# v and tau laid out in DRAM for every channel, Haar coefficients kept at true scale, and mixing's rows loaded a step earlier

## The chip, the cores and the metric

The kernel runs on one core of a Trainium2 chip. The metric is the device time of one execution in microseconds; the kernel before takes 2840.51 us (median of three runs, 2833.68 to 2842.04).

## What is computed

The input x has 4 images of 64 channels of 256 x 256 numbers in fp32. Four layers follow one another. Layers 0, 2 and 3 are long convolutions, layer 1 mixes channels in a Haar wavelet domain:

```python
# layers 0, 2, 3: k is an outer product of two learned filters per channel
y = irfft2(rfft2(x) * rfft2(k))[..., :L, :L]
x = y + x * bias[:, None, None]
# layer 1
f1 = haar2d(x)
acc = 0
for i in range(2):
    f4 = einsum('bchw,oc->bohw', f1 * v[i], conv_w[i])
    acc += sign(f4) * relu(abs(f4) - tau[i])
x = haar2d(acc, inverse=True) + x
```

v and tau have one value for each of the two branches and each of the 256 x 256 coefficients, the same for all channels. conv_w[i] is a 64 x 64 matrix over the channels. The kernel adds x in the Haar domain, so that one inverse transform serves for both. Since v is the same for all channels, it is applied after the channel matrix.

## The kernel before, in words

The filters are separable, so a convolution is two products with triangular Toeplitz matrices, one over rows and one over columns, in blocks of 64 (`toeplitz`, L303, matmuls at L307). A Haar transform of 256 is done as a product of 64 x 64 in the matmuls (`haar`, L316, matmuls at L319) for one axis and as a chain of sums and differences along the free axis for the other (`forward_free`, L334; `inverse_free`, L362).

The images are split in two groups of two. Work goes in rounds of two channels of one group, 32 rounds a group, and there are three phases.

- Phase A (`phase_a`, L427) does layer 0 and the forward transform of a round: load x (L136), products over rows (PSUM a1ps, copied by ScalarE at L451), products over columns (a2ps, with the bias added by VectorE at L471), the free axis on GpSimd (L355 and L357), the other axis on TensorE (a3ps), a copy out of PSUM into f (L484), and a store of f to DRAM as coef (L488).
- Phase B (`phase_b`, L529) mixes the channels of one group. A step takes 128 rows of coefficients, and there are 64 steps; each step has two units, one for each branch. A unit is: `mix` (matmuls with conv_w, L595), `multiply` by v (VectorE, L610), `sign` and `magnitude` (ScalarE, L614 and L618), `less` (minus tau, VectorE, L621), `threshold` (VectorE, L624), `add` (GpSimd, L636 for the second unit of a step, L639 and L640 for the first). ScalarE moves half of the rows with `exchange` (L630). A step loads ft from coef (L550) and v and tau (L556), and stores gt as mixed (L645).
- Phase C (`phase_c`, L692) loads mixed (L704), does the inverse transform, and layers 2 and 3, and stores out.

Transfers are all issued from the sync engine's queue (SP), in program order. Each engine works through its instructions in the order in which the program emits them. That order is written out by hand: every phase is a list of small pieces, and `beside` (L822) emits the pieces of a main phase with those of a side list spread evenly between them. While phase A works on group 1, phase B mixes group 0; while phase C works on group 0, phase B mixes group 1. Phase A of group 0 has the filter networks and their spreading to DRAM beside it (`rest`, L291). Phase C of group 1 runs alone at the end. Evacuations of PSUM in phases A and C are put off by `later` (L401) to the beginning of the next piece.

In phase B, piece (u, j) with j = 0, 1, 2 does the parts of unit u that `piece` (L648) lists: in j = 0 the multiply of u, `less` of u - 1 and `add` of u - 2; in j = 1 the matmuls of u + 1. At j = 1 of a step's first unit the loads of step s + 2 are issued, and at j = 2 of its second unit the store of step s - 1. The buffers are 4 for ft, 3 each for v, tau, m and gt, 2 for x, and one PSUM tile each for the matmul's result and for a.

The Haar butterflies are done without the factors of the square root of a half, and the coefficients lie in DRAM unscaled. Their scale is instead put into tau: `scale_tau` (L264) multiplies tau by the inverse scale along both axes, and `copy_tau` (L271) writes the result to a DRAM tensor, taus, in eight copies. v comes from the host in eight copies too. Both are read with a step of zero over the 8 channels that share a copy:

```python
at = src.offset + s * 4 * W * COPIES
flat = bass.AP(src.tensor, at, [[2 * W, 2 * COPIES], [0, C // COPIES], [1, 2 * W]])
```

The first rows of the transform, which hold sums over all blocks, are treated apart: `join` (L564) at the beginning of mixing, on VectorE, and `part` (L576) before the first store, on GpSimd.

Of the kernel before, what the change touches and what calls it, by code (L numbers as in the profile page):

```python
# [41 lines left out]
F32 = mybir.dt.float32  # L42
AF = mybir.ActivationFunctionType
ALU = mybir.AluOpType
# [3 lines left out]
P = 128  # L48
B, C, N = 4, 64, 256

ROW = 64
# [8 lines left out]

FIRST = 2

COPIES = 8

GROUPS = 2
NB = B // GROUPS
CI = 4 // NB
# [22 lines left out]

@with_exitstack
def conv_haar_kernel(
    ctx: ExitStack, tc: tile.TileContext, x, zT, w1, wbd, cols, decay, wo_first, decay_first, bias, forward, inverse, wcol, wrow, pack, v, tau, out
):
    nc = tc.nc
    ctx.enter_context(tc.manual_schedule())
# [9 lines left out]
    coef = [coefficients(f"coef{g}") for g in range(GROUPS)]  # L106
    mixed = [coefficients(f"mixed{g}") for g in range(GROUPS)]
    filt = [dram.tile([P, REPEATS, PERIOD], F32, tag=f"filt{l}", name=f"filt{l}") for l in range(NL)]

    taus = dram.tile([C, 2, COPIES, 2, W], F32, tag="taus", name="taus")  # L110


    def pool(name, bufs, stack=ctx, **kw):
        return stack.enter_context(tc.tile_pool(name=name, bufs=bufs, reuse_waits="tile", **kw))
# [50 lines left out]
    def constant(name, src, shape):  # L165
        t = mp.tile(shape, F32, tag=name, name=f"{name}_sb")
        nc.sync.dma_start(t, src)
        return t
# [89 lines left out]
    thresholds = []  # L258

    def load_tau():  # L260
        thresholds.append(constant("wrow", wrow.partition_broadcast(P), [P, N]))
        thresholds.append(constant("tau", tau, [P, 4, N]))

    def scale_tau():  # L264
        wrow_sb, tau_sb = thresholds
        nc.vector.tensor_tensor(tau_sb, tau_sb, wrow_sb.unsqueeze(1).to_broadcast([P, 4, N]), ALU.mult)
        for h in range(2):
            half = tau_sb.rearrange("p (i h) k -> p i h k", h=2)[:, :, h, :]
            nc.vector.tensor_scalar(half, half, wcol_sb[:, h : h + 1], None, ALU.mult)

    def copy_tau(k):  # L271
        tau_sb = thresholds[1]
        for i in range(2):
            to = bass.AP(taus.tensor, taus.offset + (k * 2 + i) * W, [[2 * W * COPIES, P], [1, W]])
            nc.sync.dma_start(to, tau_sb[:, 2 * i : 2 * i + 2].rearrange("p h k -> p (h k)"))
# [6 lines left out]
    wcol_sb = const.tile([P, 2], F32, tag="wcol", name="wcol_sb")  # L282
    nc.sync.dma_start(wcol_sb, wcol)
    bias_sb = const.tile([P, NL * C], F32, tag="bias", name="bias_sb")
    nc.sync.dma_start(bias_sb, bias.partition_broadcast(P))

# [1 line left out]
        p()  # L288

    thirds = [slice(0, 7), slice(7, 14), slice(14, REPEATS)]  # L290
    rest = [load_tau] + [lambda q=q, k=k: spread(0, q, k) for q in range(1, 4) for k in thirds]  # L291
# [3 lines left out]
    rest.append(scale_tau)  # L295
    rest += [lambda k=k: copy_tau(k) for k in range(COPIES)]

    TILES = [(r, c) for r in range(2) for c in range(2)]

# [62 lines left out]
    def inverse_free(src, dst, name, engine):  # L362


        blocks = src.rearrange("p n (k q) -> p n k q", k=BLOCKS)

        def diffs(half):
            if half < BLOCKS:
                return blocks[:, :, half : 2 * half, 0]
            m = half // BLOCKS  # L370
            return src.rearrange("p n (k q) -> p (n k) q", k=BLOCKS)[:, :, m : 2 * m]

        def scale(half):
            if half < N and engine is nc.gpsimd:
                nc.scalar.mul(diffs(half), diffs(half), float(half))  # L375

        cur, half = blocks[:, :, 0:1, 0], 1
        while half < N:
            scale(2 * half)
            o = dst  # L380
            if half < HALF:
                o = ac.tile([P, 2 * M, 2 * half], F32, tag=f"h{2 * half}", name=f"{name}{2 * half}", bufs=1)
            d = diffs(half)
            if half < BLOCKS:
                s, pair = cur, o.rearrange("p n (t q) -> p n t q", q=2)
            else:
                s = cur.rearrange("p n (k t) -> p (n k) t", k=BLOCKS)
                pair = o.rearrange("p n (k t q) -> p (n k) t q", k=BLOCKS, q=2)
            for q, op in ((0, ALU.add), (1, ALU.subtract)):
                to = pair[:, :, :, q]  # L390
                if engine is nc.gpsimd:
                    engine.tensor_tensor(to, s, d, op)  # L392
                else:
                    engine.scalar_tensor_tensor(to, d, float(half) * (1 - 2 * q), s, ALU.mult, ALU.add)
                yield
            cur = o
            half *= 2
# [3 lines left out]
    def later(op):  # L401

        waiting.append(op)
# [23 lines left out]
    def phase_a():  # L427
# [45 lines left out]
        def product(t, bp):  # L473
            s = st[t]
            if bp == 0:

                s["f"] = big("out", f"f_{t}", 2)
            two = banks(f"a3ps{bp}_{t}")
            fw = blocks(s["fw"])
            haar(two, lambda r, c: fw[half(r), c, 2 * bp : 2 * bp + 2], forward_sb)  # L480
            for b, ps in enumerate(two):
                f = s["f"][:, 4 * bp + 2 * b : 4 * bp + 2 * b + 2]
                copy = nc.vector.tensor_copy if b and t < ROUNDS else nc.scalar.copy
                later(lambda f=f, ps=ps, copy=copy: copy(f, ps))  # L484

        def store(t):
            for to, f in all_rows(coef[t // ROUNDS], t % ROUNDS, st[t]["f"]):
# [41 lines left out]
    def phase_b(grp):  # L529
# [11 lines left out]
            at = [ap.offset + (e * STEPS // 2 + s // 2) * PAIR + s % 2 * P // CI * n for e in range(CI)]  # L541
            return [(bass.AP(ap.tensor, at[e], [[n, P // CI], [1, n]]), by_e[e]) for e in range(CI)]

        def load(s):
            if s >= STEPS:
                return
            d = st[s]
            d["f"] = bp.tile([P, NB, W], F32, tag="ft", name=f"ft_{grp}_{s}", bufs=4)
            for rows, f in step_of(coef[grp], s, d["f"]):
                nc.sync.dma_start(f, rows)  # L550
            for name, src in (("v", v), ("tau", taus)):
                t = d[name] = bp.tile([P, 2, W], F32, tag=name, name=f"{name}_{grp}_{s}", bufs=3)

                at = src.offset + s * 4 * W * COPIES
                flat = bass.AP(src.tensor, at, [[2 * W, 2 * COPIES], [0, C // COPIES], [1, 2 * W]])
                nc.sync.dma_start(t.rearrange("p e w -> p (e w)"), flat)  # L556

        def four(name, at, b):

# [4 lines left out]
        def join(image):  # L564

            a, b, c, d, t, u = four("f", half(image), image)
            op = nc.vector.tensor_tensor
            op(t, a, b, ALU.add)
            op(b, a, b, ALU.subtract)
            op(u, c, d, ALU.add)  # L570
            op(d, c, d, ALU.subtract)
            nc.vector.tensor_copy(c, b)
            op(a, t, u, ALU.add)
            op(b, t, u, ALU.subtract)

        def part():  # L576

            a, b, c, d, t, u = four("g", half(0), slice(0, NB))
            op = nc.gpsimd.tensor_tensor
            op(t, a, b, ALU.add)  # L580
            op(b, a, b, ALU.subtract)
            op(u, c, c, ALU.add)
            op(a, t, u, ALU.add)
            op(d, d, d, ALU.add)
            op(c, b, d, ALU.add)
            op(d, b, d, ALU.subtract)
            op(b, t, u, ALU.subtract)
# [55 lines left out]
        def store(s):  # L643
            for to, g in step_of(mixed[grp], s, st[s]["g"]):
                nc.sync.dma_start(to, g)  # L645
            st[s].clear()

        def piece(u, j):  # L648

            s, i = divmod(u, 2)  # L650
            if j == 0:
                if u < units:
                    multiply(u)
                if 0 < u <= units:
                    less(u - 1)
                if 1 < u <= units + 1:
                    add(u - 2)
            elif j == 1:
                if u + 1 < units:
                    mix(u + 1)  # L660
                if u < units:
                    sign(u)
                if 0 < u <= units:
                    threshold(u - 1)
                if i == 0 and s > 0:
                    load(s + 2)
            else:
                if u < units:
                    magnitude(u)
                if i == 0 and s < STEPS:  # L670
                    exchange(s)
                if i and s > 0:

                    if s == 2:
                        part()
                        store(0)
                    if s > 1:
                        store(s - 1)
# [12 lines left out]

    def phase_c():  # L692
# [277 lines left out]
```

## Time and profile before

| What | Before |
| --- | --- |
| Time | 2840.51 us (2833.68 to 2842.04) |
| Span of the profiled execution | 2849.9 us, clock of TensorE 0.941 of full |
| TensorE busy | 2429.2 us (85%) |
| VectorE (DVE) busy | 1582.2 us (56%), 1779 instructions |
| ScalarE (ACT) busy | 1427.8 us (50%), 2361 instructions |
| GpSimd (POOL) busy | 1947.6 us (68%), 2422 instructions |
| DMA engines, main queue | 71.5% of 16 engines, 628.64 MB |
| HBM read, written | 413.12 MB, 215.35 MB |

A line of a group in the profile names the source line, the engine, the operation, the output and the inputs, and the count; then the busy time in us, the mean ns of one, the idle time of the engine just before, and what ended most of it. A line of waits names who waited, for whom, the total in us, how many times, and the longest. PEld is the loading of weights. SPq is the sync engine's queue. "issue" is time for which the profile shows no cause. The page gives shares over the whole span; the stages have different limits, so a table of busy time by stretches is read beside it.

### The profile page before, as it was taken

What the parts mean: (1) busy time and instruction counts of PE and PEld (TensorE: products, weight loads), DVE (VectorE), ACT (ScalarE), POOL (GpSimd) and SP (SyncE); (2) the same over time, 40 slices, a digit from 0 to 9 for tenths busy, and PEclk for the clock granted to TensorE, in tenths of its full rate; (3) what the DMA queues carried; (4) which work ended last, traced back from release to release, by engine and by line L of the source; (5) the groups of instructions that cost most, each with busy time, mean ns of one, the idle gap of its engine ahead of it and who ended that gap; (6) DMA issues with size and microseconds to landing.
All of it is one profiled execution on the core that took longest, in us unless ns stands there. A gap on an engine that the chain in (4) does not pass through costs nothing.

```text
span 2849.9 us, 120142 instructions
## 1 busy us (share of the span) xinstructions
PE 2429.2 (85%) x53276; PEld 1931.0 (68%) x53276; DVE 1582.2 (56%) x1779; ACT 1427.8 (50%) x2361; POOL 1947.6 (68%) x2422
## 2 busy tenths in 40 slices
PE   6999998667677676769888888888889999999999
PEld 5777776444444454547676767676667888888888
DVE  2353336777677777527776767676763333333333
ACT  1222224666656566426675666675763333333332
POOL 2787777977778787648777777776765555555561
PEclk9999999988988888879999999999999999999999
DMA  5668887989989998666888888887885444444432
GB/s 156 219 212 262 239 283 245 274 280 283 277 268 294 280 286 276 207 186 195 257 263 244 270 259 240 257 258 230 259 245 184 146 145 149 142 158 134 158 118 93
DMA packets 243773, 636.31 MB, mean 223 GB/s; under 512 B 43174, under 2 KB 125767, under 8 KB 227128
## 3 DMA queue, kind: packets, MB, share of 16 engines
q1 hardware_dynamic: 243256, 628.64, 71.5%
q8 instruction: 419, 6.86, 1.0%
q14 instruction: 98, 0.80, 0.1%
HBM read 413.12 MB, written 215.35 MB: 221 GB/s over the span
## 4 chain that ended last, share of the span: by engine, by line
PE 40%; DMA 23%; DVE 9%; ACT 5%; POOL 4%; issue 3%; SPq 3%; DVEq 0%; ACTq 0%; POOLq 0%
PE c1c L307 8%; PE c2r L307 8%; PE c2c L307 7%; PE c1r L307 6%; DMA ft<-coef 6%; DMA v<-in_v 4%; DMA tau<-taus 4%; PE f L595 3%; PE c0ps L319 3%; DMA x<-in_x 3%; DVE a L621 2%; DMA mixed<-gt 2%; DVE x L610 2%; DMA g<-mixed 2%; PE a2ps L307 1%
## 5 line engine op out<-in xcount | busy, mean ns | idle before, releaser
L392 POOL TENSOR_TENSOR i<-i,g 128x16 f32<-128x16 f32 x744 | 394.5, 550 | 489.3 <-ACT g L375 476.6
L595 PE MATMUL f<-ft,mix 64*64 64x512 f32 x2048 | 341.3, 687 | 262.2 <-DMA ft<-coef 180.5
L610 DVE TENSOR_TENSOR x<-f,v 128x1024 f32<-128x1024 f32 x256 | 312.0, 1219 | 267.0 <-PE f L595 140.4
L307 PEld LDWEIGHTS a1ps<-tx,x 64*64 64x64 f32 x8192 | 322.5, 142 | 121.5 <-issue 61.7
L307 PE MATMUL a1ps<-tx,x 64*64 64x192 f32 (+3 forms) x8192 | 354.2, 315 | 34.6 <-issue 11.2
L614 ACT ACTIVATE m<-x 128x1024 f32<-128x1024 f32 x256 | 272.0, 1063 | 209.9 <-DVE x L610 151.7
L307 PEld LDWEIGHTS c2r<-tx,cy 64*64 64x64 f32 x8192 | 307.6, 137 | 92.0 <-ACT ch L745 53.9
L307 PEld LDWEIGHTS c1c<-ty,ch 64*64 64x64 f32 x8192 | 300.9, 133 | 90.2 <-ACT ch L745 53.1
L307 PEld LDWEIGHTS a2ps<-ty,ay 64*64 64x64 f32 x8192 | 308.1, 140 | 70.8 <-issue 44.3
L307 PE MATMUL c2r<-tx,cy 64*64 64x256 f32 (+3 forms) x8192 | 341.6, 306 | 11.8 <-ACT ch L745 6.5
L307 PE MATMUL c1c<-ty,ch 64*64 64x192 f32 (+3 forms) x8192 | 330.3, 299 | 22.8 <-issue 12.7
L307 PE MATMUL a2ps<-ty,ay 64*64 64x256 f32 (+3 forms) x8192 | 340.8, 311 | 8.5 <-issue 7.8
L621 DVE TENSOR_TENSOR a<-a,tau 128x1024 f32<-128x1024 f32 x256 | 313.8, 1226 | 60.9 <-ACT a L618 60.5
L618 ACT ACTIVATE a<-x 128x1024 f32<-128x1024 f32 x256 | 264.8, 1034 | 162.3 <-DVE m L624 161.7
L307 PE MATMUL c1r<-tx,z 64*64 64x64 f32 (+3 forms) x8192 | 329.9, 302 | 12.5 <-ACT g L375 6.8
L307 PEld LDWEIGHTS c1r<-tx,z 64*64 64x64 f32 x8192 | 306.8, 136 | 49.8 <-issue 28.8
L636 POOL TENSOR_TENSOR gt<-gt,m 128x1024 f32<-128x1024 f32 x128 | 303.1, 2368 | 44.9 <-DVE m L624 41.8
L745 ACT COPY ch<-c1r 128x512 f32<-128x512 f32 x256 | 137.2, 588 | 390.5 <-PE c1r L307 390.1
L471 DVE SCALAR_TENSOR_TENSOR x<-x,bias_sb,a2ps 128x512 f32<-128x512 f32 x256 | 179.4, 742 | 268.2 <-PE a2ps L307 243.1
L307 PE MATMUL c2c<-ty,ch 64*64 64x192 f32 (+3 forms) x8192 | 319.3, 298 | 9.2 <-issue 9.2
L624 DVE SCALAR_TENSOR_TENSOR m<-a,m 128x1024 f32<-128x1024 f32 x256 | 313.0, 1223 | 22.1 <-DVE a L621 0.5
L307 PEld LDWEIGHTS c2c<-ty,ch 64*64 64x64 f32 x8192 | 300.5, 134 | 32.3 <-issue 18.4
(71 smaller groups left out, 3193.1 us busy)
## 6 DMA issues: line engine op xcount, KB each, us to landing
coef<-f SPq DMA_DIRECT2D x256, 256.0 KB, 4.1
ft<-coef SPq DMA_DIRECT2D x256, 256.0 KB, 6.8
v<-in_v SPq DMA_DIRECT2D x128, 512.0 KB, 7.5
tau<-taus SPq DMA_DIRECT2D x128, 512.0 KB, 8.5
mixed<-gt SPq DMA_DIRECT2D x256, 256.0 KB, 7.2
g<-mixed SPq DMA_DIRECT2D x256, 256.0 KB, 5.9
x<-in_x SPq DMA_DIRECT2D x63, 1024.0 KB, 8.5
out<-o SPq DMA_DIRECT2D x63, 1024.0 KB, 5.0
```

The source lines that it names most:

```text
L307: nc.tensor.matmul(ps[r][half(c), j % 2, k * ROW :], data[half(r), c, k, bass.ts(j, ROW)], t(r, c)[:, : N - k * ROW], start=k == 0, stop=k ...
L319: nc.tensor.matmul(ps[r][half(c)].rearrange("p h k -> p (h k)"), matrix[half(r)], pairs(r, c).rearrange("p h k -> p (h k)"), start=True, s ...
L392: engine.tensor_tensor(to, s, d, op)
L471: nc.vector.scalar_tensor_tensor(to, old, bias_sb[:, c : c + 1], ps, ALU.mult, ALU.add)
L595: nc.tensor.matmul(un[u]["f4"][half(q), b, :], mixers[0][half(r), bass.ts(i, C)], st[s]["f"][half(r), b], start=True, stop=True, tile_posi ...
L610: nc.vector.tensor_tensor(un[u]["x"], un[u]["f4"], both(u, "v"), ALU.mult)
L614: nc.scalar.activation(un[u]["m"], un[u]["x"], AF.Sign)
L618: nc.scalar.activation(un[u]["a"], un[u]["x"], AF.Abs)
L621: nc.vector.tensor_tensor(un[u]["a"], un[u]["a"], both(u, "tau"), ALU.subtract)
L624: nc.vector.scalar_tensor_tensor(un[u]["m"], un[u]["a"], 0.0, un[u]["m"], ALU.max, ALU.mult)
L636: nc.gpsimd.tensor_tensor(st[s]["g"], st[s]["g"], m, ALU.add)
L745: later(lambda y=y, ps=ps: nc.scalar.copy(y, ps))
```

## The change

There are four parts.

1. v and tau come from the host with a copy for each of the 64 channels, and a step's rows are 128 distinct rows one after another in DRAM. The tensor taus, `load_tau`, `scale_tau` and `copy_tau` go.
2. Coefficients are at true scale along both axes, so tau needs no scaling. The host's matrix `forward` carries the scale along one axis. Along the other the scale is multiplied in as f leaves PSUM: a tensor_tensor by a broadcast row `wrow_sb`, always on VectorE, where f was copied by ScalarE, or for the second of two tiles in the first 32 rounds by VectorE. The inverse uses the square root of `half` in place of `half`, and `join` and `part` multiply by the square root of two.
3. `load` is split: `load_v` stays at step s + 2, and `load_f` asks for step s + 3, after `load_v` in the queue. At the start of mixing, four ft are asked for ahead of v and tau.
4. The store of step s - 1 moves from the last piece of step s to the first piece of step s + 1, behind that piece's `add`. A last piece is appended for it.

```diff
-COPIES = 8
...
-    taus = dram.tile([C, 2, COPIES, 2, W], F32, tag="taus", name="taus")
...
-    def load_tau():
...
-    def scale_tau():
...
-    def copy_tau(k):
...
+    wrow_sb = const.tile([P, N], F32, tag="wrow", name="wrow_sb")
+    nc.sync.dma_start(wrow_sb, wrow.partition_broadcast(P))
...
-                nc.scalar.mul(diffs(half), diffs(half), float(half))
+                nc.scalar.mul(diffs(half), diffs(half), math.sqrt(half))
...
-                copy = nc.vector.tensor_copy if b and t < ROUNDS else nc.scalar.copy
-                later(lambda f=f, ps=ps, copy=copy: copy(f, ps))
+                w = wrow_sb.unsqueeze(1).to_broadcast([P, 2, N])
+                later(lambda f=f, ps=ps, w=w: nc.vector.tensor_tensor(f, ps, w, ALU.mult))
...
-        def load(s):
+        def load_f(s):
             if s >= STEPS:
                 return
             d = st[s]
             d["f"] = bp.tile([P, NB, W], F32, tag="ft", name=f"ft_{grp}_{s}", bufs=4)
             for rows, f in step_of(coef[grp], s, d["f"]):
                 nc.sync.dma_start(f, rows)
-            for name, src in (("v", v), ("tau", taus)):
+
+        def load_v(s):
+            if s >= STEPS:
+                return
+            n = 2 * W
+            d = st[s]
+            for name, src in (("v", v), ("tau", tau)):
                 t = d[name] = bp.tile([P, 2, W], F32, tag=name, name=f"{name}_{grp}_{s}", bufs=3)
 
-                at = src.offset + s * 4 * W * COPIES
-                flat = bass.AP(src.tensor, at, [[2 * W, 2 * COPIES], [0, C // COPIES], [1, 2 * W]])
-                nc.sync.dma_start(t.rearrange("p e w -> p (e w)"), flat)
+                rows = bass.AP(src.tensor, src.offset + s * P * n, [[n, P], [1, n]])
+                nc.sync.dma_start(t.rearrange("p e w -> p (e w)"), rows)
...
-            nc.vector.tensor_copy(c, b)
+            nc.vector.tensor_scalar(c, b, math.sqrt(2.0), None, ALU.mult)
+            nc.vector.tensor_scalar(d, d, math.sqrt(2.0), None, ALU.mult)
...
-            op(u, c, c, ALU.add)
+            nc.gpsimd.tensor_scalar(u, c, math.sqrt(2.0), None, ALU.mult)
...
-            op(d, d, d, ALU.add)
+            nc.gpsimd.tensor_scalar(d, d, math.sqrt(2.0), None, ALU.mult)
...
                 if 1 < u <= units + 1:
                     add(u - 2)
+                if i == 0 and s > 2:
+
+                    if s == 3:
+                        part()
+                        store(0)
+                    store(s - 2)
...
                 if i == 0 and s > 0:
-                    load(s + 2)
+
+                    load_v(s + 2)
+                    load_f(s + 3)
...
-                if i and s > 0:
-
-                    if s == 2:
-                        part()
-                        store(0)
-                    if s > 1:
-                        store(s - 1)
...
+            for s in range(4):
+                load_f(s)
             for s in range(3):
-                load(s)
+                load_v(s)
...
+        pieces.append(lambda: piece(units + 2, 0))
...
+    signs = signs * w[order][:ROW, None]
...
-        "v": f(np.repeat(v[:, :, None], COPIES, axis=2)),
-        "tau": f(by_row("tau").reshape(P, 4, N)),
+        "v": f(np.repeat(v[:, :, None], C, axis=2)),
+        "tau": f(np.repeat(by_row("tau")[:, :, None], C, axis=2)),
```

More of the change, by code (lines that the diff above doesn't have):

```diff
@@ L92, in conv_haar_kernel @@
 def conv_haar_kernel(
-    ctx: ExitStack, tc: tile.TileContext, x, zT, w1, wbd, cols, decay, wo_first, decay_first, bias, forward, inverse, wcol, wrow, pack, v, tau, out
+    ctx: ExitStack, tc: tile.TileContext, x, zT, w1, wbd, cols, decay, wo_first, decay_first, bias, forward, inverse, wrow, pack, v, tau, out
 ):
@@ L256, in spread @@
             nc.sync.dma_start(filt[l][s, part], src.to_broadcast([src.shape[0], times, PERIOD]))
-    thresholds = []
-    def load_tau():
-        thresholds.append(constant("wrow", wrow.partition_broadcast(P), [P, N]))
-        thresholds.append(constant("tau", tau, [P, 4, N]))
-    def scale_tau():
[L265 to L269, printed above, removed]
-    def copy_tau(k):
[L272 to L275, printed above, removed]
     first_x = [load_x(0)]
@@ L281, in conv_haar_kernel @@
     nc.sync.dma_start(inverse_sb, inverse)
-    wcol_sb = const.tile([P, 2], F32, tag="wcol", name="wcol_sb")
-    nc.sync.dma_start(wcol_sb, wcol)
+    wrow_sb = const.tile([P, N], F32, tag="wrow", name="wrow_sb")
+    nc.sync.dma_start(wrow_sb, wrow.partition_broadcast(P))
     bias_sb = const.tile([P, NL * C], F32, tag="bias", name="bias_sb")
@@ L290, in conv_haar_kernel @@
     thirds = [slice(0, 7), slice(7, 14), slice(14, REPEATS)]
-    rest = [load_tau] + [lambda q=q, k=k: spread(0, q, k) for q in range(1, 4) for k in thirds]
+    rest = [lambda q=q, k=k: spread(0, q, k) for q in range(1, 4) for k in thirds]
     rest.append(lambda: wbd_sb.extend(constant(f"wbd{l}", wbd[:, l], [P, 3, P]) for l in (1, 2)))
@@ L294, in conv_haar_kernel @@
     rest += [lambda l=l, q=q, k=k: spread(l, q, k) for l in (1, 2) for q in range(4) for k in thirds]
-    rest.append(scale_tau)
-    rest += [lambda k=k: copy_tau(k) for k in range(COPIES)]
     TILES = [(r, c) for r in range(2) for c in range(2)]
@@ L393, in inverse_free @@
                 else:
-                    engine.scalar_tensor_tensor(to, d, float(half) * (1 - 2 * q), s, ALU.mult, ALU.add)
+                    engine.scalar_tensor_tensor(to, d, math.sqrt(half) * (1 - 2 * q), s, ALU.mult, ALU.add)
                 yield
@@ L915 @@
     signs[0] = 1.0
-    scaled = signs * w[order][:ROW, None] ** 2 / N
+    scaled = signs * w[order][:ROW, None] / math.sqrt(N)
+    signs = signs * w[order][:ROW, None]
     pack = a["L1_conv_conv_w"].transpose(2, 0, 1).reshape(C, P)
@@ L951 @@
         "inverse": f(np.concatenate([scaled] * 2).astype(np.float32)),
-        "wcol": f((1 / w)[order].reshape(2, 2, ROW // 2, 2).transpose(2, 0, 3, 1).reshape(P, 2).astype(np.float32)),
-        "wrow": f((1 / w)[order].astype(np.float32)),
+        "wrow": f(w[order].astype(np.float32)),
         "pack": f(np.concatenate([pack, pack])),
-        "v": f(np.repeat(v[:, :, None], COPIES, axis=2)),
-        "tau": f(by_row("tau").reshape(P, 4, N)),
+        "v": f(np.repeat(v[:, :, None], C, axis=2)),
+        "tau": f(np.repeat(by_row("tau")[:, :, None], C, axis=2)),
     }
```

## The prediction

> **What bounds the kernel now.** I read the table by stages first, then the waits inside each stage, then the costliest groups and the DMA issues. The stages, in us: A filters group 0 (to about 455), A filters group 1 beside B mixing group 0 (to about 1210), C finishes group 0 beside B mixing group 1 (about 1290 to 2130), C finishes group 1 alone. Busy time by stretch; the last three columns are the granted clock, DMA share and GB/s:
>
> ```profile
> core 0: us, PE busy (x) PEld busy (x) DVE busy (x) ACT busy (x) POOL busy (x), PEclk, DMA share, GB/s
> 0.00:356.00 356.00, 313.53 (x7196) 257.85 (x7196) 133.51 (x203) 90.41 (x163) 240.17 (x406) 0.98 0.71 218
> 700.00:900.00 200.00, 138.69 (x2289) 88.97 (x2284) 147.20 (x138) 125.05 (x168) 156.04 (x176) 0.87 0.92 276
> 1500.00:1700.00 200.00, 173.72 (x3724) 139.47 (x3716) 142.73 (x145) 131.88 (x211) 145.65 (x149) 0.95 0.85 256
> 2200.00:2850.00 650.00, 643.41 (x16976) 574.46 (x16966) 224.91 (x321) 239.19 (x524) 339.78 (x473) 1.00 0.43 138
> ```
>
> The outer stages are TensorE's (88% and 99%). In the first mixing stage TensorE has 69%, DVE 74%, POOL 78%, and the DMA engines 92%: DMA is the bound. In the second TensorE has 87% and DMA 85%. The waits from 500 to 1180 (total, times, longest), then from 1320 to 2100:
>
> ```profile
> PE f L595 <- DMA ft<-coef: 128.8, 43, 5.7
> DVE x L610 <- DMA v<-in_v: 83.7, 29, 6.6
> DVE x L610 <- PE f L595: 47.0, 23, 4.1
> ```
>
> ```profile
> DVE x L610 <- PE f L595: 91.0, 30, 9.0
> PE f L595 <- DMA ft<-coef: 49.6, 14, 6.6
> DVE x L610 <- DMA v<-in_v: 38.0, 9, 7.7
> ```
>
> Mixing's matmuls wait for rows of coefficients, its multiply for v. The sync queue waits too, for DMA's own progress: in the first stretch
>
> ```profile
> SPq L149 <- DMA v<-in_v: 28.6, 19, 2.0
> SPq L149 <- DMA ft<-coef: 28.5, 45, 2.0
> SPq L149 <- DMA tau<-taus: 26.8, 20, 2.0
> ```
>
> so loads back up behind loads. Which transfer is too dear? The issues (KB, median us to landing):
>
> ```profile
> v<-in_v SPq DMA_DIRECT2D x128, 512.0 KB, 7.5
> tau<-taus SPq DMA_DIRECT2D x128, 512.0 KB, 8.5
> x<-in_x SPq DMA_DIRECT2D x63, 1024.0 KB, 8.5
> ```
>
> v and tau take as long as an x of twice their size. The trace's records of single packets say more. Packets of 4096 bytes have a mean of 166 ns in the opening stage (stores of coef) and 171 in the closing one (loads of g). From 500 to 1100 there are 33,196: median 159, mean 213, and 36% above 200 ns. By counts (a step moves 128 each of ft, v, tau and mixed; a round 256 of coef) v and tau are about 41% of them. In the first loads of mixing, near 456 us, the eight ft packets of an engine take 159 each but for the first, and the sixteen of v and tau after them mostly 240 to 360. If the others cost 167, v and tau cost (213 - 0.585 x 167) / 0.415 = 278 ns. What sets them apart: eight partitions read one row of DRAM.
>
> [...]
>
> **The change part by part.**
> v and tau for every channel. Same bytes into SBUF, each row read once. A packet falls from 278 to between 167 (ft, g) and 190 (half of the 380 mean of x's 8 KB packets, contiguous in DRAM). I take 178: 100 ns less x 16 packets an engine = 1.6 us of DMA a step. From 500 to 1180 there are 61 steps (122 units), 11.15 us each; DMA's 0.92 x 11.15 = 10.3 us falls to 8.7.
>
> f scaled on the way out of PSUM, all on DVE. Per round four 128x512 tensor_tensor in place of four ACT copies (two ACT, two DVE in group 0):
>
> ```profile
> L484 ACT COPY f<-a3ps 128x512 f32<-128x512 f32 x192 | 106.2, 587 | 240.8 <-issue 147.4 <-PE a3ps L319 87.7 <-DMA filt<-padded 4.7
> L484 DVE COPY f<-a3ps 128x512 f32<-128x512 f32 x64 | 43.9, 688 | 18.3 <-PE a3ps L319 17.2
> L471 DVE SCALAR_TENSOR_TENSOR x<-x,bias_sb,a2ps 128x512 f32<-128x512 f32 x256 | 179.4, 742 | 268.2 <-PE a2ps L307 243.1
> ```
>
> Bounds 688 and 742 ns; I take 0.70 us. In the first mixing stage 100 such copies leave ACT: DVE gains 70 us, in 680. DVE was busy 73% (497 us), so it has 567. Of its 183 us of idle, v's 83.7 and 70% of the 47 behind the mixing matmul (129 of that matmul's 187 us of idle are DMA) are DMA's: 117. The other 66 stay: 567 + 66 = 633, that is -47. POOL's load, about 9.0 us a step (4.9 adding, 0.41 rounds of 9.9), is then 87%, and PSUM waits on a busier DVE; I give 12 back: -35. Bounds: -47, and 0 if DVE's queue eats it all.
>
> In the opening stage two copies in a row on DVE (1.4 us) follow two residuals (1.5) where ACT and DVE shared them; TensorE's next rows need those banks. Its weight loads wait 29 us there for such residuals already. I take 0.15 us a round x 33 = +5; bounds 0 and +16.
>
> Second mixing stage: no f there. TensorE idles 110 of 780 us; ft's 49.6 and some 10 through late multiplies are DMA's. All gone would be -60, none 0; with POOL, ACT and DVE all near 75% of a shorter stage I take -40.
>
> Rows a step further ahead: ft is asked for five units before its matmul instead of three (28 us against 17; it lands in 6.8), and at the start four f go ahead of v: join's second rows waited 6.9 and 5.5 us, of which I count -5. The added wait: the load of f(s+3) takes the buffer of s-1, last read by POOL's add (L639), queued just before. Behind it in the sync queue stand toeplitz rows, x or g, coef or out, and the next v. The queue has room: a step issues about 10.5 DMAs at 0.57 us, 6 of 11 us (second stage 7.8 of 13.4). Near 810 us the L639 in question ends at 810.6, the L621 that tau's load waited for anyway at 811.4. So 0; at worst 1 us a step while waiting, still inside the slack. Stores move one piece later: POOL has had longer, and gt's three buffers leave two steps: 0.
>
> Gone: 16 stores of taus, a load, three DVE operations (about 6 us), in a stage TensorE bounds: 0. Other scale factors, join's one more operation and POOL's multiplies: eight small operations, about 2 us in all, on DVE and POOL while TensorE works on A or C: 0.
>
> Sum: -35 - 40 - 5 + 5 = -75, 2840 - 75 = 2765.
>
> **Rivals.**
> DVE becomes the bound: the first mixing stage gives nothing back (the 70 us on DVE take up what the loads free), the second 25: 2815. For: DVE 73% to 83% before any shortening. Against: two thirds of its idle is DMA's.
> Both stages come down to their other limits: -47 - 60 - 10 = 2723. For: TensorE's clock is 0.87 and 0.95 there and could rise. [...]
> Slower: the packets are slow by load, not by repetition. Then DVE's 70 us stay, half exposed (+35), +5 in the opening: 2880. For: x packets, read once, also average 380 ns against a median of 309. Against: ft packets beside them in the first loads ran at 159.
>
> **How the numbers follow.** Forecast 0.60 (2740 to 2795), DVE bound 0.15 (2795 to 2838), more 0.14 (2690 to 2740), slower 0.11. Leaving out the slow case and the far end of the third gives 2700 to 2840. Below 2832 (0.3%): 0.60 + 0.14 and most of DVE's case, 0.86; within 0.3% 0.03; slower 0.11. Prediction 2765.
>
> **What would show it.** 4 KB packets near 170 to 190 on average and DMA near 0.8 in the first mixing stage; L595's wait for ft and L610's for v nearly gone; DVE above 85% there; f on DVE near 0.70 us; the closing stage unchanged. Wrong if packets stay above 200, if TensorE waits for DVE's f instead, or if the sync queue waits long for POOL at the load of f.

## The result, and the profile after

The changed kernel takes 2677.30 us (median of 4 runs, 2676.37 to 2693.52) beside 2840.86 for the kernel before (2833.68 to 2842.04). The ratio is 0.9443, with a 95% interval of 0.9404 to 0.9482. It is 164 us faster. The forecast was 75 us, and the time lies below the stated range of 2700 to 2840. The later runs took place beside further executions of the kernel before, with medians of 2845.64 to 2848.56 us (one at 2861.76), so the ratios are what to compare among them; the 95% interval of each stands in brackets behind its ratio.

Busy time by stretch of the changed kernel, with the columns of the table of before (the last three are the granted clock, the DMA share and GB/s):

```profile
core 0: us, PE busy (x) PEld busy (x) DVE busy (x) ACT busy (x) POOL busy (x), PEclk, DMA share, GB/s
0.00:356.00 356.00, 312.56 (x6913) 248.68 (x6917) 155.96 (x242) 60.30 (x111) 230.81 (x390) 0.98 0.63 206
700.00:900.00 200.00, 159.74 (x2669) 99.58 (x2663) 190.54 (x195) 129.90 (x162) 180.69 (x203) 0.95 0.90 331
1500.00:1700.00 200.00, 186.56 (x4140) 155.38 (x4136) 156.26 (x158) 151.38 (x245) 163.36 (x169) 0.98 0.82 291
2050.00:2676.00 626.00, 620.59 (x16360) 554.01 (x16352) 217.92 (x311) 230.77 (x504) 327.91 (x456) 1.00 0.43 137
```

In this stretch of the first mixing stage DVE went from 74% to 95% busy and POOL from 78% to 90%. The DMA engines stay busy (0.90, and 0.92 before), but they move 331 GB/s in place of 276. In the second, TensorE went from 87% to 93%, in the stretches around it to 96%, at a clock of 0.98 to 1.00 in place of 0.95 to 0.97. The closing stage is as it was.

In the changed kernel the matmuls of mixing stand in L575, `multiply` in L590, `sign` and `magnitude` in L594 and L598, `less` and `threshold` in L601 and L604, `add` in L616, L619 and L620; f is written in L458, and L281 has the products of the convolutions. Three of the longest waits of the changed kernel from 510 to 1090, the first mixing stage (total us, times, longest):

```profile
ACT a L598 <- DVE m L604: 110.1, 84, 2.5
PEld f L575 <- DVE x L590: 100.2, 87, 3.7
PE f L575 <- DVE x L590: 81.4, 70, 3.6
```

and its DVE's alone:

```profile
DVE a L601 <- ACT a L598: 33.0, 29, 8.1
DVE x L445 <- PE a2ps L281: 1.5, 1, 1.5
```

DVE's list is whole, and neither it nor TensorE's has a wait for ft or v any more. Before, the matmul's wait for ft (128.8 us) and the multiply's for v (83.7) stood there; now others wait for DVE. From 1260 to 1940, the second mixing stage, the longest waits of TensorE's matmuls are short:

```profile
PE c2r L281 <- ACT ch L729: 11.3, 8, 2.4
PE c0ps L293 <- ACT ch L729: 4.9, 5, 1.8
PE c0ps L293 <- POOL ci L366: 4.8, 1, 4.8
```

The issues of v, tau and x (KB, median us to landing), and the weight loads of phase A's first product over the whole span:

```profile
v<-in_v SPq DMA_DIRECT2D x128, 512.0 KB, 6.0
tau<-in_tau SPq DMA_DIRECT2D x128, 512.0 KB, 6.5
x<-in_x SPq DMA_DIRECT2D x63, 1024.0 KB, 5.6
```

```profile
L281 PEld LDWEIGHTS a1ps<-tx,x 64*64 64x64 f32 x8192 | 316.3, 139 | 135.2 <-DVE f L458 75.5
```

v, tau and x all land sooner (7.5, 8.5 and 8.5 before). x gained though nothing about it was changed. In the first mixing stage alone its median fell from 11.5 to 8.3 us, and it is 10.5 with the repeated rows put back (a_rep8, below), so there x gains mainly because the loads beside it are quicker. The last line shows where part 2 is felt: these weight loads now wait 75.5 us for DVE's f, where before they waited 22.8 for ScalarE's and 6.4 for DVE's. What that costs, an experiment below tells.

**Where the time went.** I divided every trace at three events: the first load of ft, the last store of coef, and the last multiply by v. That gives four stages. "4 KB" is the mean ns of the packets of 4096 bytes in the inner part of the first and of the second mixing stage, and "half clock" the time in the two mixing stages in which TensorE's clock record stands at 0.5.

| Run | opening | mixing 1 | mixing 2 | tail | span | 4 KB | half clock |
| --- | --- | --- | --- | --- | --- | --- | --- |
| before | 453.2 | 797.2 | 878.3 | 721.2 | 2849.9 | 212, 221 | 215, 96 |
| changed | 466.5 | 717.6 | 773.8 | 718.1 | 2676.0 | 176, 177 | 119, 27 |
| b_layout | 503.0 | 729.7 | 786.3 | 722.4 | 2741.4 | 185, 179 | 140, 34 |
| b_order | 447.5 | 774.2 | 852.5 | 717.8 | 2792.0 | 217, 220 | 201, 75 |
| b_layout_order | 504.0 | 716.1 | 774.9 | 718.0 | 2713.0 | 175, 177 | 133, 38 |
| a_old_order | 464.8 | 728.7 | 783.4 | 722.7 | 2699.6 | 186, 178 | 123, 38 |
| a_rep8 | 463.5 | 782.2 | 856.0 | 719.3 | 2821.0 | 219, 220 | 218, 72 |
| a_split16 | 464.0 | 717.8 | 776.8 | 718.7 | 2677.3 | 176, 178 | 123, 31 |
| a_rep4 | 464.0 | 720.7 | 777.9 | 719.9 | 2682.5 | 179, 178 | 113, 34 |
| a_rep2 | 466.6 | 717.9 | 777.3 | 718.9 | 2680.7 | 176, 177 | 133, 31 |
| a_f_copied | 452.8 | 716.3 | 776.4 | 718.5 | 2664.0 | 177, 176 | 130, 31 |
| a_pool_less | 469.5 | 705.0 | 777.3 | 720.2 | 2672.0 | 176, 179 | 109, 27 |
| a_fc_pool_less | 457.2 | 690.0 | 783.1 | 719.5 | 2649.8 | 175, 178 | 102, 38 |
| a_m4 | 471.6 | 702.6 | 778.6 | 719.8 | 2672.6 | 177, 177 | 116, 34 |

The change gave 80 us in the first mixing stage, 104 in the second and 3 in the tail, and took 13 in the opening. That is 174 in all and not 164, because the traced execution of the kernel before took 2851.65 us, 11 above its median. Each line is one execution. How far such figures scatter can be seen from the changed kernel, a_split16, a_rep2 and a_rep4, whose times lie within 8 us: their stages agree within about 3 us in the opening and the first mixing stage and within about 4 in the second.

### The profile page after: what moved, and what is told of

The parts are those of the page before. It is cut to its first block, busy times and chain, and to the rows that moved or that the text cites. A ratio compares the mean times of both kernels' runs of the same rounds, so it can differ in the third digit from the quotient of the medians.

```text
span 2676.0 us, 120070 instructions
## 1 busy us (share of the span) xinstructions
PE 2415.2 (90%) x53276; PEld 1912.8 (71%) x53276; DVE 1684.8 (63%) x1972; ACT 1327.5 (50%) x2169; POOL 1951.0 (73%) x2422
## 4 chain that ended last, share of the span: by engine, by line
PE 51%; DVE 14%; POOL 11%; DMA 9%; ACT 7%; issue 6%; SPq 2%; DVEq 0%; POOLq 0%; ACTq 0%
PE c2r L281 9%; PE c1c L281 9%; PE c1r L281 7%; PE c2c L281 7%; PE a1ps L281 6%; PE a2ps L281 6%; PE c0ps L293 3%; DVE a L601 3%; PE a3ps L293 3%; POOL f L331 3%; DVE x L590 3%; POOL fw L329 3%; POOL gt L616 2%; PE f L575 2%; DVE m L604 2%
## 5 line engine op out<-in xcount | busy, mean ns | idle before, releaser
L575 PE MATMUL f<-ft,mix 64*64 64x512 f32 x2048 | 321.7, 638 | 106.2 <-DVE x L590 86.5
L281 PEld LDWEIGHTS a1ps<-tx,x 64*64 64x64 f32 x8192 | 316.3, 139 | 135.2 <-DVE f L458 75.5
L281 PE MATMUL a1ps<-tx,x 64*64 64x192 f32 (+3 forms) x8192 | 360.9, 311 | 37.1 <-DVE f L458 17.9
L281 PEld LDWEIGHTS c2r<-tx,cy 64*64 64x64 f32 x8192 | 310.0, 135 | 87.7 <-ACT ch L729 61.2
L598 ACT ACTIVATE a<-x 128x1024 f32<-128x1024 f32 x256 | 265.0, 1035 | 206.1 <-DVE m L604 205.8
L601 DVE TENSOR_TENSOR a<-a,tau 128x1024 f32<-128x1024 f32 x256 | 314.1, 1227 | 80.3 <-ACT a L598 78.1
L594 ACT ACTIVATE m<-x 128x1024 f32<-128x1024 f32 x256 | 272.2, 1063 | 171.7 <-DVE x L590 108.8
L281 PE MATMUL c2r<-tx,cy 64*64 64x256 f32 (+3 forms) x8192 | 343.3, 303 | 15.2 <-ACT ch L729 11.3
L281 PEld LDWEIGHTS c1c<-ty,ch 64*64 64x64 f32 x8192 | 303.6, 133 | 74.8 <-ACT ch L729 57.7
L590 DVE TENSOR_TENSOR x<-f,v 128x1024 f32<-128x1024 f32 x256 | 311.1, 1215 | 55.9 <-PE f L575 52.6
L281 PEld LDWEIGHTS a2ps<-ty,ay 64*64 64x64 f32 x8192 | 295.9, 135 | 68.4 <-issue 31.1
L281 PE MATMUL a2ps<-ty,ay 64*64 64x128 f32 (+3 forms) x8192 | 326.3, 301 | 15.3 <-ACT ay L425 8.5
L281 PE MATMUL c1c<-ty,ch 64*64 64x128 f32 (+3 forms) x8192 | 332.2, 299 | 8.2 <-ACT ch L729 7.5
L281 PE MATMUL c1r<-tx,z 64*64 64x128 f32 (+3 forms) x8192 | 328.0, 299 | 10.4 <-DMA tx<-filt 6.5
L425 ACT COPY ay<-a1ps 128x512 f32<-128x512 f32 x256 | 137.3, 588 | 401.8 <-PE a1ps L281 401.4
L281 PEld LDWEIGHTS c1r<-tx,z 64*64 64x64 f32 x8192 | 302.0, 134 | 43.7 <-issue 23.7
L604 DVE SCALAR_TENSOR_TENSOR m<-a,m 128x1024 f32<-128x1024 f32 x256 | 312.7, 1222 | 19.4
L281 PE MATMUL c2c<-ty,ch 64*64 64x256 f32 (+3 forms) x8192 | 318.4, 297 | 3.9 <-issue 3.8
L281 PEld LDWEIGHTS c2c<-ty,ch 64*64 64x64 f32 x8192 | 301.8, 133 | 24.3 <-issue 11.5
L616 POOL TENSOR_TENSOR gt<-gt,m 128x1024 f32<-128x1024 f32 x128 | 303.4, 2370 | 11.9 <-DVE m L604 10.3
```

The costliest lines, as they stand in the source:

```text
L281: nc.tensor.matmul(ps[r][half(c), j % 2, k * ROW :], data[half(r), c, k, bass.ts(j, ROW)], t(r, c)[:, : N - k * ROW], start=k == 0, stop=k ...
L425: later(lambda y=y, ps=ps: nc.scalar.copy(y, ps))
L575: nc.tensor.matmul(un[u]["f4"][half(q), b, :], mixers[0][half(r), bass.ts(i, C)], st[s]["f"][half(r), b], start=True, stop=True, tile_posi ...
L590: nc.vector.tensor_tensor(un[u]["x"], un[u]["f4"], both(u, "v"), ALU.mult)
L594: nc.scalar.activation(un[u]["m"], un[u]["x"], AF.Sign)
L598: nc.scalar.activation(un[u]["a"], un[u]["x"], AF.Abs)
```

## The experiments

Two theories stood against each other at first. L: the rows that eight partitions read cost DMA time, and all else follows. O: asking for the rows earlier, and storing later, is what frees the queue. Four runs take one part out or put one part in alone.

**Layout alone, put into the kernel before (b_layout).**

```diff
-COPIES = 8
+COPIES = 64
...
-                flat = bass.AP(src.tensor, at, [[2 * W, 2 * COPIES], [0, C // COPIES], [1, 2 * W]])
+                flat = bass.AP(src.tensor, at, [[2 * W, P], [1, 2 * W]])
```

> The kernel before with only the layout of v and tau changed: 64 copies of each in DRAM (tau still scaled on the chip, written by 8 transfers of 8 rows per partition), read as 128 distinct rows; f is copied as before, rows and stores are issued as before. Theory L (the repeated rows are the cost, all else follows): packets of 4 KB average under 185 ns in both mixing stages, time 2610 to 2700, at or below the changed kernel since DVE is spared f. Theory O (asking for the rows a step earlier and storing later is what frees the queue): 2770 or more, the waits for ft stay above 80 us.

Measured 2744.27 us, ratio 0.9640 (0.9609 to 0.9671). The total lies in neither theory's range. One reason lies outside the mixing: the opening stage took 503 us in place of 453. The copies of tau are written there, 64 in place of 8, as 8 transfers of 4096 KB issued between 364 and 466 us. The trace shows what they do: from 400 to 440 the DMA engines are busy throughout at 398 GB/s, and TensorE works 18.4 of these 40 us, where it works 38.1 in the kernel before. The mixing stages fell by 68 and 92 us, to within 13 of the changed kernel's, and the second's packets average 179 ns, the first's 185. The wait for ft in the first (560 to 1150) is down to 49.0 us, under the 80 that theory O had named, but it is not gone, and 34.1 us of the multiply's wait for v stay too. The layout alone does most, not all.

**Order alone, put into the kernel before (b_order).**

```diff
+                if i == 0 and s > 2:
...
+                    store(s - 2)
...
-                    load(s + 2)
+                    load_v(s + 2)
+                    load_f(s + 3)
...
-                if i and s > 0:
...
-                        store(s - 1)
...
+            for s in range(4):
+                load_f(s)
             for s in range(3):
-                load(s)
+                load_v(s)
```

> The kernel before with only the order of mixing's transfers changed: rows of coefficients a step further ahead, stores one piece later, four of them first at the start; v and tau still in eight copies, f copied as before. Theory L: the DMA engines stay 0.9 busy in the first mixing stage and the time falls by less than 40 us (2800 to 2840); waits for ft move over to v. Theory O: 2700 to 2750.

Measured 2800.13 us, ratio 0.9831 (0.9797 to 0.9864): between the theories, nearer to L, which had allowed a fall of 40 us where 48 came. The mixing stages fell by 23 and 26 us. The packets are as slow as before (217 and 220 ns). Two waits from 500 to 1160 in this run, whose L600 is the matmuls of mixing and L615 the multiply:

```profile
PE f L600 <- DVE x L615: 130.7, 71, 4.8
DVE x L615 <- DMA v<-in_v: 107.6, 47, 4.8
```

The matmul's wait for ft is gone and the multiply waits for v in its stead, 107.6 us where it waited 83.7. Asking earlier for one load mostly moved the wait to the next.

**The old order, put into the changed kernel (a_old_order).**

> The changed kernel with mixing's rows and stores issued where they were before. Theory L: 2675 to 2700, waits for ft under 40 us. Theory O: 2760 or more, with the matmuls waiting over 100 us for ft.

The edit is the reverse of the last. Measured 2712.11 us, ratio 0.9529 (0.9495 to 0.9563), 12 us above theory L's range and far below theory O's. The mixing stages are 11 and 10 us longer than in the changed kernel. In its first, from 510 to 1100, TensorE waits for ft again, but for 35.5 us, not 128.8:

```profile
PE f L575 <- DMA ft<-coef: 35.5, 17, 4.2
```

**Eight copies again, in the changed kernel (a_rep8).**

```diff
+COPIES = 8
...
-                rows = bass.AP(src.tensor, src.offset + s * P * n, [[n, P], [1, n]])
+                at = src.offset + s * 2 * COPIES * n
+                rows = bass.AP(src.tensor, at, [[n, 2 * COPIES], [0, C // COPIES], [1, n]])
...
-        "v": f(np.repeat(v[:, :, None], C, axis=2)),
-        "tau": f(np.repeat(by_row("tau")[:, :, None], C, axis=2)),
+        "v": f(np.repeat(v[:, :, None], COPIES, axis=2)),
+        "tau": f(np.repeat(by_row("tau")[:, :, None], COPIES, axis=2)),
```

> The changed kernel with v and tau in eight copies, each row read by eight partitions, as before; all else as changed. Theory L: packets of 4 KB average over 205 ns in the mixing stages, DMA 0.9 busy, time 2810 to 2880. Theory O: 2680 to 2730.

Measured 2825.50 us, ratio 0.9923 (0.9896 to 0.9950). Everything else of the change is in, and only 23 us are gained over the kernel before, as theory L expected. The packets are at 219 and 220 ns, and from 700 to 900 the DMA engines are 97% busy at 298 GB/s:

```profile
700.00:900.00 200.00, 157.37 (x2416) 100.10 (x2420) 173.95 (x178) 117.73 (x147) 163.87 (x182) 0.85 0.97 298
```

Theory O falls. Theory L holds for the greater part, though not all else follows from the layout. The layout is worth 65 and 82 us in the two stages when it is taken out, 68 and 92 when it is put in alone; the order 11 and 10 when it is taken out, 23 and 26 when it is put in alone. Together they make 80 and 104, less than the two single parts added. The waits of b_order say why: both parts work on the same waits for loads.

**Repetition, or the shape of the transfer?** The old transfer also described its source as 16 blocks of 8 rows, so that shape could be the cost, and not the repetition. One run keeps the distinct rows and takes that shape back; two more have 32 and 16 copies, so that two and four partitions read a row, with the edit of a_rep8.

```diff
-                rows = bass.AP(src.tensor, src.offset + s * P * n, [[n, P], [1, n]])
+                rows = bass.AP(src.tensor, src.offset + s * P * n, [[8 * n, 16], [n, 8], [1, n]])
```

> The changed kernel with the same distinct rows of v and tau, but the source described as 16 blocks of 8 rows, the shape that the transfers had before. Theory L (the repeated row costs): nothing changes, 4 KB packets 175 to 185 ns, 2670 to 2700. Rival S (the shape[...] costs): packets over 205 ns and 2800 or more.

> The changed kernel with 32 copies of v and tau: each row is read by two partitions in a row. Theory L with a cost that grows with the repeats: 4 KB packets 185 to 200 ns, time 2690 to 2760. If any repeat is as dear as eight: over 210 ns and about 2825. If two cost nothing: 177 ns and 2675.

> The changed kernel with 16 copies of v and tau, each row read by four partitions in a row; eight cost 44 ns a packet on the mean of all 4 KB packets and two cost nothing. If the cost grows evenly between them: packets near 190 ns and 2700 to 2750. If it begins only past four: 176 ns and 2675 to 2690. If four are as dear as eight: over 210 ns and about 2825.

Measured, one run each: 2679.46 us with 176 and 178 ns for the shape (a_split16), 2682.78 us with 176 and 177 ns for two (a_rep2), 2684.62 us with 179 and 178 ns for four (a_rep4). The shape costs nothing that can be seen, so the repetition is what costs. But it doesn't cost evenly: one, two and four partitions to a row are alike within 3 ns, and eight cost 43 more on the mean of all 4 KB packets of the first mixing stage. The shares say the same more sharply: in that stage 35% of the 4 KB packets took over 200 ns before, 6.5% in the changed kernel, 6.6% with four partitions to a row and 45% with eight. I had expected a slope. Why it begins between four and eight stays open; these runs don't tell.

**What bounds the first mixing stage now?** By the busy shares it looks like DVE (95% from 700 to 900), theory D; GpSimd at 90% is the rival, G. First, f copied as before:

```diff
-                later(lambda f=f, ps=ps, w=w: nc.vector.tensor_tensor(f, ps, w, ALU.mult))
+                copy = nc.vector.tensor_copy if b and t < ROUNDS else nc.scalar.copy
+                later(lambda f=f, ps=ps, copy=copy: copy(f, ps))
```

> The changed kernel with f copied out of PSUM as before (ScalarE, and every second one by VectorE in the first 32 rounds): it leaves out the scale along the second axis, so only its time counts. Theory D (VectorE, 95% busy, is the bound of the first mixing stage): that stage shortens by 40 us or more from 718, the opening stage by 10 from 466, time 2610 to 2635. Rival G (GpSimd and the order of the queues bound it as much): the stage stays within 15 us of 718 and only the opening stage gains, 2655 to 2670.

> The kernel before with the layout of v and tau and with the order of mixing's transfers changed, and f still copied as before: everything but the true scale. Its opening stage carries the writes of 64 copies of tau, some 50 us in the run with the layout alone. If layout and order add up as the two single runs say (first mixing stage 730 less 11, second 786 less 10) it takes 2715 to 2730; theory D expects the first mixing stage under 680 and 2680 or less, since here VectorE has no f beyond the copies of before.

Measured 2664.51 us for a_f_copied, ratio 0.9362 (0.9320 to 0.9404), and 2711.35 us for b_layout_order, ratio 0.9526 (0.9490 to 0.9563). Theory D falls as stated: without the 96 multiplications for f, which take 61.1 us from 510 to 1090 (DVE's busy time falls from 536 to 487 us), the stage takes 716.3 us, and without the true scale altogether 716.1, against 717.6. DVE's time went into a longer wait for ScalarE (33.0 us in the changed kernel), and ScalarE's sign waits longer for GpSimd. From 510 to 1090 in the changed kernel

```profile
ACT m L594 <- POOL gt L616: 31.3, 23, 3.1
```

and in a_f_copied

```profile
DVE a L601 <- ACT a L598: 68.5, 48, 8.1
ACT m L594 <- POOL gt L616: 57.0, 34, 3.3
ACT m L594 <- POOL gt L620: 19.3, 19, 2.5
```

The opening stage, though, fell from 466.5 to 452.8: moving f to DVE cost 14 us there, where TensorE is the bound (88% busy from 0 to 356) and the weight loads of its next rows wait for DVE's f (32.5 us from 20 to 440 in the changed kernel). b_layout_order adds up the two single parts nearly as its expectation had it (716.1 and 774.9 us in the mixing stages for 719 and 776; the whole is 4 us under the stated range), and shows that layout and order are the whole gain of the mixing stages. Its opening again carries the writes of tau: 504 us. That is what part 2 is worth. It costs 14 us in the opening, and it spares the writing of 64 copies of tau on the chip.

Then GpSimd with less to do, with DVE as it is (a_pool_less) and relieved too (a_fc_pool_less, which has the edit above as well):

```diff
-                nc.gpsimd.tensor_tensor(g[:, 1], m[:, 1], st[s]["other"], ALU.add)
+                nc.scalar.copy(g[:, 1], st[s]["other"])
```

and, with all the work kept, a fourth buffer for m (a_m4):

```diff
-        tx = ac.tile([P, CI, N], F32, tag="tx", name=f"tx{l}_{t}", bufs=5)
+        tx = ac.tile([P, CI, N], F32, tag="tx", name=f"tx{l}_{t}", bufs=4)
...
-            un[u]["m"] = bp.tile([P, NB, W], F32, tag="m", name=f"m_{grp}_{u}", bufs=3)
+            un[u]["m"] = bp.tile([P, NB, W], F32, tag="m", name=f"m_{grp}_{u}", bufs=4)
```

> The changed kernel with less work on GpSimd: the first unit's add for the second image (1.28 us a step) is left out, and a ScalarE copy of 0.6 us writes that half of gt instead, so branch 0 is missing from the second image. Theory G (GpSimd, 91% busy, bounds the first mixing stage through the m buffers that ScalarE's sign waits for): the stage falls by 30 us or more from 718. Theory D (VectorE, 95% busy, bounds it too): it stays within 15 us, since f is still on VectorE. Second mixing stage, bound by TensorE: within 10 us of 774.

> The same with f also copied out of PSUM as before, so both VectorE and GpSimd have less to do (the second axis' scale and branch 0 of the second image are left out). If VectorE and GpSimd bound the stage together, only this one of the three falls: 718 to 680 or less. If GpSimd alone bounds it, this one and the one before fall alike. If neither does (TensorE, or the order of the queues), it stays near 716.

> The changed kernel with four m buffers in place of three, and, to make room, four tx buffers in place of five. Theory G's way of acting (sign waits for GpSimd to free m, 52 us of ScalarE's waits in the first mixing stage): those waits fall under 15 us and the stage by 5 to 25 us. If GpSimd's throughput itself is the bound, the waits go and the stage stays within 5 us of 718. If four tx are too few, the tail of 718 us grows.

Measured, the first two with two runs each: a_pool_less 2676.80 us, ratio 0.9403 (0.9349 to 0.9456), first mixing stage 705.0; a_fc_pool_less 2648.89 us, ratio 0.9305 (0.9252 to 0.9357), stage 690.0; a_m4 2674.42 us, ratio 0.9388 (0.9346 to 0.9431), stage 702.6. DVE relieved gives 1 us, GpSimd relieved 13, both 28. None of the outcomes named ahead came in full: 13 is short of theory G's 30 and inside the 15 of theory D, which had fallen already, and both together stop 10 us short of 680. Still, the two together give twice what they give one by one, so neither is the bound alone: they are both close to it. The waits above say that each is held by the other through ScalarE, and in a_m4 this can be seen. From 510 to 1080 sign's wait for L616, 31.3 us in the changed kernel, is

```profile
ACT m L594 <- POOL gt L616: 1.8, 1, 1.8
```

and the stage is 15 us shorter, as theory G's way of acting would have it. That a_fc_pool_less stops at 690 and not 680 says that a third limit may be near. Two stand ready, and no run takes either away: the DMA engines are 91% busy from 510 to 1050 in that run, and ScalarE, which got the work that the other two lost, is 79% busy there, against 63% from 510 to 1090 in the changed kernel. a_m4 can't be told from the changed kernel in the whole time (their intervals overlap: its opening was 5 us longer), so no version here that does all the work beats it beyond doubt.

## Why the prediction was wrong, point by point

The direction and the cause were right, and most of the side effects; the size was off, in the price of f in the first mixing stage and in the floor of the second. The busy times behind both:

```profile
500.00:1180.00 680.00, 476.50 (x7726) 306.40 (x7722) 498.85 (x466) 423.40 (x566) 535.77 (x591) 0.86 0.91 280
1320.00:2100.00 780.00, 668.93 (x14359) 534.17 (x14351) 548.28 (x554) 516.90 (x828) 578.27 (x591) 0.95 0.84 250
```

before, and in the changed kernel

```profile
510.00:1090.00 580.00, 456.44 (x7480) 278.93 (x7480) 536.29 (x549) 364.02 (x452) 521.36 (x571) 0.92 0.87 317
1260.00:1940.00 680.00, 643.83 (x14290) 527.57 (x14294) 541.62 (x547) 518.71 (x835) 570.72 (x588) 0.99 0.82 291
```

- **v and tau for every channel.** Right in cause (a_rep8, b_layout). The packets of v and tau fell from 278 ns to about (176 - 0.585 x 167) / 0.415 = 189 by the same reckoning, an estimate that gives every other packet 167 ns; it is the upper end of the 167 to 190 that I gave. That DMA would come down to near 0.8 busy was wrong: it is at 0.87 from 510 to 1090, because the stage runs faster. A step there takes 580 / 59.5 = 9.75 us in place of 11.15.
- **The first mixing stage, -35; measured -80.** The sum was -117 for DVE's idle that leads back to loads, +70 for f and +12 given back. The runs measure its terms. Layout and order without f on DVE (b_layout_order) take the stage from 797.2 to 716.1 us, that is -81, and f on top makes it 717.6 (changed), that is +1.5. The failed step is f's full price, "567 + 66": f's 70 us were added to DVE's work, and 66 us of idle were to stay beside it. They did not stay. From 510 to 1090, for 59.5 steps, DVE works 536 of 580 us in the changed kernel and waits 33.0 for ScalarE; in a_f_copied it does the same steps in the same time, works 487 and waits 68.5 for ScalarE. So f's work went into idle time that the stage has in any case, because GpSimd and ScalarE hold it too. The other two terms erred the opposite way, -81 where they made -105: as the loads came in time, DVE's wait for ScalarE took their place in part, from 23.9 us before (500 to 1180) to 70.0 in b_layout_order (550 to 1130). Only a part of the first error was cancelled by the second.
- **The second mixing stage, -40 with a floor of -60; measured -104.** The failed step is the floor itself: "ft's 49.6 and some 10 through late multiplies are DMA's". Of 780 us for 58 steps (1320 to 2100) TensorE worked 669 and idled 111; afterwards 58 steps take 680 us (1260 to 1940), of which it works 644 and idles 36. So 75 us of idle went, and not 60 at most. Sums over its waits show which: those for DMA fell from 51 us to none, and those for which the profile names no cause ("issue") from 34 to 8. I had left these 34 standing. Two runs show that they hang on the packets, too. With the repeated rows but the new order (b_order from 1290 to 2050, a_rep8 from 1310 to 2070) the waits named DMA's are nearly gone as well, 5 and 2 us, but TensorE still waits 91 and 99 us: 28 and 27 for DVE, 37 and 42 without a named cause. With the new layout alone (b_layout from 1300 to 1990) it waits 43 in all.
- **The same stage, the clock.** The other 25 us came out of TensorE's busy time, which I had held fixed: the time at half clock fell from 96 to 27 us in the stage. The clock record of before knows only 0.5 and 1, and 43 of its 69 low stretches last 3.413 us. In the 3.413 us ahead of a low stretch TensorE was busy 25% of the time on the mean, and 65% at most, against 77% from 470 to 1900 us. So low stretches followed stalls; what turns the clock down and up again, no run here shows. Over the whole trace a 64x512 matmul takes 1073 ns on the mean inside a low stretch and 610 otherwise. From 1320 to 2100 TensorE worked 64 us at half clock before, and from 1260 to 1940 13 us afterwards; by that ratio 51 us of slow work less are worth about 22 of the 25, an estimate. By these figures stalls were paid twice here, as idle and as slow work after them, and a forecast that takes stalls away has to count both. I had named the clock only in a rival.
- **The opening stage, +5 of 0 to 16; measured +13.** The mechanism was right and a_f_copied isolates it. The weight loads of a1ps wait 32.5 us for DVE's f from 20 to 440, where they waited 12.9 for the f of both engines before. I had given 0.15 us a round, and about 0.4 came.
- **f in the mixing stage.** 0.679 us each, and it costs nothing there (a_f_copied). The rival "DVE becomes the bound" named the engine that is now the busiest there, at 95%, and drew the wrong end from it.
- **Rows a step ahead, and the added wait.** The wait of the sync queue for the add (L619) at the load of f came true, 18.9 us in 12 times, and no harm from it can be seen: with the order alone both mixing stages got shorter. Order is worth 11 and 10 us in place of the -5 that I gave; what it gives beyond that when it comes alone (23 and 26) is time that the layout also frees.

The rival "both stages come down to their other limits" at 2723 was the nearest, and still 46 us too high. It charged f in full in the first stage, and it had no more than the 60 us of idle to win in the second.

## What to carry to other kernels

Where many waits lead back to one overloaded resource, the idle time that the profile puts down to it is not yet its price. In the second mixing stage, which TensorE bounds (93% busy from 1500 to 1700 in the changed kernel), more went than that: 51 us of waits for DMA, but 75 us of TensorE's idle in all, with waits for engines that were themselves late and waits without a named cause, and the time at half clock fell from 96 to 27 us beside it. In the first, where no engine is the bound alone, less went, since another wait took the place of some (ScalarE's, 23.9 us before and 70.0 in b_layout_order), and 61 us of new work on the busiest engine fell into idle time and cost 1. So ask of the remaining waits what made their releaser late before calling them fixed, and before charging an engine for new work, ask whether that engine alone sets the pace of the stage. A table that many partitions read may be worth more copies in DRAM: here rows of 4 KB shared by four partitions cost nothing that one run can tell (179 ns a packet in the first mixing stage, 176 with distinct rows), and rows shared by eight cost most of the gain (219 ns, 2825.50 us). Sixteen copies would have done in this kernel (a_rep4).

## What the runs showed of the hardware that I had not expected

- A row of 4 KB read by eight partitions of one transfer costs much more (219 ns on the mean of all such packets) than one read by four (179), two (176) or one (176). The cost begins between four and eight; these runs show no slope below.
- How much slow clock a stalled TensorE collects: over the two mixing stages 311 us at half clock before, 146 after. With quicker loads the same matmuls of mixing became shorter, from 649 ns on the mean (1320 to 2100) to 605 (1260 to 1940).
- An engine at 95% busy (DVE, from 700 to 900) was not the bound alone: with 61 us of work taken off it, which lowered its busy time by 49, a stage of 718 us became 1 us shorter.
